# A three-layer CIN on one core: the fifth tile is gathered from the half tables, and the copies into the big table are issued later

## The chip, the cores and the metric

The kernel runs on one core of one Trainium2 chip. Its time is the device time of one execution in microseconds (us). Three executions took 733.25, 734.23 and 734.82 us, so the median before the change is 734.23 us. One further execution was profiled: it took 733.14 us, of which its instructions span 731.4 us; the other 1.74 us lie around the span.

Engines are named as the profile names them: PE is TensorE's matmul, PEld its weight load, DVE is VectorE, ACT ScalarE, POOL GpSimd and SP SyncE. SP computes nothing here; it only issues transfers.

## What is computed

The input x has 1024 samples, 39 fields and 64 embedding columns, in float32. The reference is

```python
def _cin_layer(Xk, X0, W, b):
    O = W.shape[0]
    Hk, Fdim = (Xk.shape[1], X0.shape[1])
    Wr = W.reshape(O, Hk, Fdim)
    return jnp.einsum('bhe,bfe,ohf->boe', Xk, X0, Wr) + b[None, :, None]
X0 = sparse_embedding
Xk = X0
outs = []
for W, b in ((W0, b0), (W1, b1), (W2, b2)):
    Xk = _cin_layer(Xk, X0, W, b)
    outs.append(Xk.sum(axis=-1))
cin_output = jnp.concatenate(outs, axis=-1)
return cin_output @ fc_w.T + fc_b
```

All three layers have 64 outputs. The last layer is only summed and multiplied by a vector, so the kernel folds its weights into a smaller form before the main loop. What is left for the main loop is a matrix product whose rows are the products x_a * x_b of pairs of fields (and x_a alone, which is a pair with a row of ones).

## The kernel before

**Blocks, steps and tiles.** The samples are worked off in 32 blocks of 32 samples. A block has 2048 columns (32 samples by 64 embedding columns). The 39 fields and a row of ones make a table of 40 rows. A pair product needs its two factors in the same partition, so for each block five tiles r of 128 by 2048 are gathered, each an arrangement of table rows on 128 partitions chosen by a list of indices (`lists`). `PAIRS` then names six pairs of tiles, (0,1), (0,2), (3,1), (3,2), (0,4), (3,4): DVE multiplies the two tiles of a pair into a product tile p, and PE multiplies p by the weights. Tile 4, the fifth, is the only one whose list holds row 39, the ones. A seventh, smaller chunk per two blocks takes two small tiles u and v of 128 by 1024.

A step is one such chunk, written (n, c): block n, chunk c. The list `steps` has (0,0) to (0,6), then (1,0) to (1,5), then (2,0) and so on, 13 for every two blocks. Counting from zero, (0,6) is step 6, (1,0) step 7, (1,4) step 11. Chunk 6 is the small one (line 221 on DVE, lines 579 and 590 on PE); all others are line 219 on DVE (128 by 2048 in one instruction, except for the first four steps, which are made by halves or quarters) and line 559 on PE.

**Order of work.** The order of each engine is written out by hand. DVE makes the product of step k+4 after PE has been given step k (`AHEAD = 4`); there are four p buffers, so DVE is at most four steps ahead. When a block is complete, `finish` puts two ACT and four DVE operations and two reductions (lines 607, 609, 620) between the products.

**Tables.** The gathers read tables in device memory. `xd[0]`, `xd[1]`, `xd[2]` hold two blocks each (2 times 40 rows of 2048 columns), in rotation; rows 39 and 79 hold ones. A table is filled from x by `load` (312 KB, pieces of 256 bytes) for each of its blocks, and by `fill_ones`. For the very first block there are two half tables, `xh[0]` and `xh[1]`, of 39 rows by 1024 columns, loaded on ACT's queue by `load_half`; tiles 0 to 3 of block 0 are gathered from these by halves. Tile 4 of block 0, the u and v tiles, and all of block 1 come from `xd[0]`. Its rows for block 0 are copied from the half tables by two transfers on SP's queue (line 396), its rows for block 1 are loaded from x by `load(1, nc.gpsimd)`.

**Queues.** POOL issues all gathers in program order (line 174): eight from the half tables with `load(1)` between the sixth and the seventh, then tile 4 of block 0, then `roll_small(0)` (u and v), then `roll(1)` (five tiles of block 1), then five small transfers of biases and a fill of ones for `xd[2]`, later the gathers of block 2 and so on. The gathers of u, v and block 1 read rows of `xd[0]`, so they wait until the copies, `load(1)` and the ones have landed. SP issues, in this order: the row of fc weights, the two copies (line 396), a fill of ones into `xd[1]`, `load(2)`, `load(3)`, and later the loads of the other blocks. The weights of chunk c are made by `weight_rows(c)` on DVE and ACT and transposed by `weight_turn(c)` on PE, with a copy by ACT (lines 543 to 545).

Of the kernel before, what the change touches and what calls it, by code (L numbers as in the profile page):

```python
# [54 lines left out]
F32 = mybir.dt.float32  # L55
# [5 lines left out]
B, F, E, H = 1024, 39, 64, 64  # L61
FH = F * H
FT = F + 1
# [3 lines left out]
NT = 5  # L67
# [9 lines left out]
SUB = 1024  # L77
# [6 lines left out]
SB = SUB // E  # L84
NBLK = B // BB
NTAB = 3
NY = 3
# [60 lines left out]
def cin_kernel(ctx: ExitStack, tc: tile.TileContext, x, w0t, b0, w1, b1, w2, b2, fc_w, fc_b, out):  # L148
    nc = tc.nc
# [3 lines left out]
    const = ctx.enter_context(tc.tile_pool(name="const", bufs=1))  # L153
    dram = ctx.enter_context(tc.tile_pool(name="dram", bufs=1, space=DRAM))
# [3 lines left out]

    xv = x.rearrange("b f e -> f b e")
    xd = [dram.tile([2 * FT, BLK], F32, name=f"xd{k}") for k in range(NTAB)]  # L160
    xh = [dram.tile([F, SUB], F32, name=f"xh{k}") for k in range(2)]

    def bank(name):
        return psum.tile([128, MM], F32, name=name, tag="po")

    def load(n, engine=nc.sync):
        first = n % 2 * FT
        engine.dma_start(  # L168
            xd[n // 2 % NTAB][first : first + F].rearrange("f (b e) -> f b e", e=E),
            xv[:, n * BB : (n + 1) * BB, :],  # L170
        )

    def gather_rows(dst, table, k):
        nc.gpsimd.indirect_dma_start(  # L174
            dst, None, table, bass.IndirectOffsetOnAxis(ap=lists[:, k : k + 1], axis=0)
        )

    def roll(n, tiles=range(NT)):
        for i in tiles:
            k = n % 2 * NT + i  # L180
            gather_rows(rt[n % 2][:, i], xd[n // 2 % NTAB][: FT if k < NT else 2 * FT], k)

    def roll_small(n):
        table = xd[n // 2 % NTAB].rearrange("f (t c) -> (f t) c", c=SUB)
        for k, dst in enumerate((ut, vt)):
            gather_rows(dst[n // 2 % 2], table, 2 * NT + k)
# [6 lines left out]
    b2s = const.tile([H, 1], F32, name="b2s")  # L193
    b1s = const.tile([128, 1], F32, name="b1s")
    b0s = const.tile([128, 1], F32, name="b0s")
    fc0s = columns[:, 1:2]
    fcb = const.tile([NY * 32, 1], F32, name="fcb")
# [4 lines left out]
    rt = [const.tile([128, NT, BLK], F32, name=f"r{k}") for k in range(2)]  # L202
# [2 lines left out]

    ones = const.tile([16, 2, 128], F32, name="ones")
    ones1 = const.tile([16, 2, 128], F32, name="ones1")

    both = const.tile([128, F * FT], F32, name="both")
    pairs = const.tile([128, NCHUNK, 128], F32, name="pairs")  # L210
# [2 lines left out]
    def product(n, c, cols=slice(0, BLK), p=None):  # L213
        if p is None:
            p = prods.tile([128, BLK], F32, name="p", tag="p")
        if c < NPAIR:
            i, k = PAIRS[c]
            r = rt[n % 2]
            nc.vector.tensor_tensor(p[:, cols], r[:, i, cols], r[:, k, cols], ALU.mult)  # L219
        else:  # L220
            nc.vector.tensor_tensor(p[:, 0:SUB], ut[n // 2 % 2], vt[n // 2 % 2], ALU.mult)  # L221
        return p

    prep = tc.tile_pool(name="prep", bufs=1)
    with prep as prep:
# [24 lines left out]
        nc.sync.dma_start(fcrow, fc_w)  # L250
        def load_half(k):
            nc.scalar.dma_start(
                xh[k].rearrange("f (b e) -> b f e", e=E), x[k * SB : (k + 1) * SB]
            )

        nc.scalar.dma_start(w2s, w2.rearrange("o (s n) -> (o s) n", s=2))
        load_half(0)
        nc.scalar.dma_start(w0s, w0t.rearrange("b (s a) h -> (b s) (a h)", s=NW))
        nc.scalar.dma_start(w1s, w1.rearrange("o (s n) -> (o s) n", s=2))
# [35 lines left out]
        def new():  # L295
            used[0] += 1
            return tmp[:, used[0] - 1 : used[0]]
# [14 lines left out]
        for i in range(NT):  # L312
            at = OFFSET[i] - 3 * K + (0 if i < NT - 1 else -F)
# [54 lines left out]
        def fill_ones(k, engine, src):  # L368
            engine.dma_start(xd[k][F::FT].rearrange("r (p c) -> p r c", c=128), src)

        fill_ones(0, nc.gpsimd, ones)


        nc.vector.tensor_scalar(unit, apart, 0, None, ALU.is_equal)
        for h in (0, H):
            rows = slice(h, h + H)
# [3 lines left out]
        r, most, seat, far = (new() for _ in range(4))  # L380
# [8 lines left out]
        halves = [slice(0, SUB), slice(SUB, BLK)]  # L389
        for k, cols in enumerate(halves):  # L390
            for i in range(4):
                gather_rows(rt[0][:, i, cols], xh[k], i)
                if k and i == 1:
                    load(1, nc.gpsimd)
        for k in (1, 0):
            nc.sync.dma_start(xd[0][0:F, halves[k]], xh[k])
        roll(0, (4,))

# [70 lines left out]
        nc.vector.tensor_tensor(both_of[:, 0:1], most, jumps[:, 0:1], ALU.add)  # L471
        nc.vector.tensor_tensor(both_of[:, 1:2], both_of[:, 0:1], jumps[:, 1:2], ALU.add)
        nc.vector.tensor_scalar(lists[:, 2 * NT :], both_of, 2.0, seat, ALU.mult, ALU.add)
        roll_small(0)
        roll(1)
        for h in (0, H):
            nc.gpsimd.dma_start(b0s[h : h + H], b0.rearrange("(h o) -> h o", o=1))
        nc.gpsimd.dma_start(b1s, b1.rearrange("(h o) -> h o", o=1).to_broadcast([H, 2]))
        nc.gpsimd.dma_start(b2s, b2.rearrange("(h o) -> h o", o=1))
        nc.gpsimd.dma_start(  # L480
            fcb, fc_b.rearrange("(p o) -> p o", o=1).to_broadcast([NY * 32, 1])
        )
        fill_ones(2, nc.gpsimd, ones)
        w1v = w1s.rearrange("o (h f) -> o h f", f=F)
        groups = [(k, min(NA * k, F - NA)) for k in range(4)]
        for k, a in groups:
# [43 lines left out]
    def spread(c):  # L530
        for n in (SQUARE, 2 * SQUARE):
            nc.scalar.copy(pairs[:, c, n : 2 * n], pairs[:, c, 0:n])
# [3 lines left out]
    def weight_turn(c):  # L536
        place = len(turned) % 4 * 128
        if not place:
            tr = bank("tr")
        else:  # L540
            tr = turned[-1]
        turned.append(tr)
        nc.tensor.transpose(tr[:, place : place + 128], pairs[:, c], unit)  # L543
        nc.scalar.copy(wa[:, c, 0 : 2 * H], tr[:, place : place + 2 * H])  # L544
        nc.scalar.copy(wa[:, c, 2 * H :], tr[:, place : place + H])
# [5 lines left out]
    def open_block(n):  # L551
        if n not in po:
            po[n] = [bank("po") for _ in range(BLK // MM)]

    def multiply(n, c, p, quarters=range(BLK // MM)):
        open_block(n)
        for m in quarters:
            side = m % 2 * H
            nc.tensor.matmul(  # L559
                po[n][m],  # L560
                wa[:, c, side : side + 2 * H],
                p[:, bass.ts(m, MM)],
                start=n % 2 == 0 and c == 0,
                stop=n % 2 == 1 and c == NPAIR - 1,
            )
# [32 lines left out]
    def fields(n):  # L598
        g[n] = []
        for m in range(BLK // SUB):  # L600
            gt = work.tile([H + F, SUB], F32, name="g", tag="g")
            nc.scalar.copy(gt[H : H + F], rt[n % 2][0:F, 0, bass.ts(m, SUB)])  # L602
            g[n].append(gt)
# [56 lines left out]
    p = {}  # L660
# [18 lines left out]
    n, c = steps[3]  # L679
    weight_rows(c)  # L680
    p[n, c] = product(n, c, halves[0])
    product(n, c, halves[1], p[n, c])
    for k, (n, c) in enumerate(steps[:3]):
        multiply(n, c, p[n, c], (0,))
        if k < 2:
            weight_turn(steps[k + 1][1])
        multiply(n, c, p[n, c], (1,))

    for at, (n, c) in enumerate(steps[:-TAIL]):
        if c == 0 and 2 <= n and n + 4 < NBLK:  # L690
            load(n + 4)
        quarters = range(BLK // MM)
        if at < 3:
            quarters = quarters[2:]
        if at < NPAIR and at > 1:
            multiply(n, c, p[n, c], quarters[:1])
            weight_turn(steps[at + 1][1])
            quarters = quarters[1:]
            if at == NPAIR - 1:
                multiply(n, c, p[n, c], quarters[:2])  # L700
                weight_turn(NPAIR + 1)
                quarters = quarters[2:]
        if c == NPAIR:
            join(n, p.pop((n, c)))
        else:
            multiply(n, c, p.pop((n, c)), quarters)
        if not at:
            fields(0)
            nc.scalar.copy(ones1, ones)
            fill_ones(1, nc.sync, ones1)  # L710
            for k in (2, 3):
                load(k)
        if at == NPAIR - 2:
            weight_rows(NPAIR + 1)
            for k in (NPAIR, NPAIR + 1):
                spread(k)
        if at - 1 in over:
            finish(over[at - 1])
            fields(over[at - 1] + 1)
        if at + AHEAD < len(steps):  # L720
            n, c = steps[at + AHEAD]
            if at + AHEAD <= NPAIR:
                weight_rows(c)
            p[n, c] = product(n, c)
            if c == NPAIR - 1 and n + 2 < NBLK:
                roll(n + 2)
                if n % 2 == 0:
                    roll_small(n + 2)
                if n < 2:
                    load(n + 4, nc.gpsimd)  # L730
# [75 lines left out]
```

## Time and profile before

| what | value |
|---|---|
| profiled execution: its time / its span | 733.14 us / 731.4 us |
| median of three executions (lowest, highest) | 734.23 us (733.25, 734.82) |
| PE busy | 724.7 us, 99% of the span |
| DVE busy | 638.3 us, 87% |
| POOL busy | 397.6 us, 54% |
| ACT busy | 166.9 us, 23% |
| line 559: instructions, mean of one | 1536, 594 ns |
| line 219: instructions, mean of one | 198, 2224 ns |
| gathers of r from the big tables: count, mean on POOL | 156, 1938 ns |
| gathers of r from the half tables: count, mean on POOL | 8, 996 ns |

Busy times are unions over one engine. Matmuls are pipelined, so the mean of one instruction is longer than the distance from one to the next: in the main loop an instruction of line 559 follows another after 0.431 us (96 in 41.40 us), and a step of line 559 is 8 instructions, 3.45 us. In a line of a timeline stand the start, the time taken, the engine, the line, the operation, what is written from what, a count, and in brackets the time for which the engine stood idle before it and what ended that. POOL's time for a gather is the time in which it writes the transfer's descriptors; the data land later.

### The profile page before, as it was taken

The numbers are of one execution on the slowest core, as the hardware profiler recorded it, in microseconds if no ns is written. First come the engines' busy times: TensorE is split into PE (matmuls) and PEld (weight loads), VectorE is DVE, ScalarE is ACT, GpSimd is POOL, SyncE is SP. The second block draws the span as 40 slices with busy tenths as digits, with TensorE's granted clock in tenths as the row PEclk, the third lists the DMA queues.
The fourth block names the chain that finished last, engine by engine and source line by source line (L and its number), as shares of the span: only waits on it lengthen the run. The fifth ranks groups of instructions, "written<-read, shape, count | busy, mean of one in ns | idle before, by whom it ended". The sixth has DMA issues, their size and how long they took to land.

```text
span 731.4 us, 6351 instructions
## 1 busy us (share of the span) xinstructions
PE 724.7 (99%) x2375; PEld 316.1 (43%) x2375; DVE 638.3 (87%) x521; ACT 166.9 (23%) x240; POOL 397.6 (54%) x254
## 2 busy tenths in 40 slices
PE   8999999999999999999999999999999999999998
PEld 4444444444444444444444444444444444444443
DVE  6999798988889988889988889888898988889885
ACT  3332121222212222221222212222121221212222
POOL 6789886536555445754537555455654547545300
PEclk9999999999999999999999999999999999999999
DMA  8997899789575887757679675896767777565700
GB/s 268 376 337 280 315 342 356 290 307 338 232 273 231 281 336 286 270 225 285 269 288 330 223 289 219 304 348 236 268 256 274 301 287 266 224 252 236 288 0 0
DMA packets 65983, 197.24 MB, mean 270 GB/s; under 512 B 40110, under 2 KB 40179, under 8 KB 45984
## 3 DMA queue, kind: packets, MB, share of 16 engines
q0 software_dynamic: 28784, 185.56, 65.5%
q1 hardware_dynamic: 35468, 9.29, 5.5%
q10 hardware_dynamic: 1700, 1.99, 1.0%
q8 instruction: 18, 0.29, 0.1%
q14 instruction: 13, 0.11, 0.0%
HBM read 196.76 MB, written 10.60 MB: 284 GB/s over the span
## 4 chain that ended last, share of the span: by engine, by line
PE 99%; DVE 0%; DMA 0%; issue 0%; ACT 0%; DVEq 0%
PE po L559 91%; PE po L579 4%; PE po L590 2%; PE idle L279 0%; PE pv L406 0%; PE pt L487 0%; PE small L323 0%; PE pv L487 0%; PE pw L418 0%; DMA fcrow<-in_fc_w 0%; PE tr L543 0%; DVE g L609 0%; DVE pairs L526 0%; DVE sums L631 0%; ACT z L607 0%
## 5 line engine op out<-in xcount | busy, mean ns | idle before, releaser
L559 PE MATMUL po<-p,wa 128*128 128x512 f32 x1536 | 666.0, 594 | 0.0
L219 DVE TENSOR_TENSOR p<-r 128x2048 f32<-128x2048 f32 (+2 forms) x198 | 434.1, 2224 | 72.4 <-PE po L559 67.1
L559 PEld LDWEIGHTS po<-p,wa 128*128 128x128 f32 x1536 | 290.5, 190 | 371.7 <-issue 354.6
L174 POOL DMA_INDIRECT r<-xd,lists x156 | 302.3, 1938 | 267.1 <-issue 266.2
L607 ACT ACTIVATE z<-po,columns 64x512 f32<-64x512 f32 x128 | 87.3, 682 | 380.1 <-PE po L590 217.9
L609 DVE SCALAR_TENSOR_TENSOR g<-po,b0s,z 64x512 f32<-64x512 f32 x128 | 95.9, 749 | 9.3 <-ACT z L607 5.3
L602 ACT COPY g<-r 39x1024 f32<-39x1024 f32 x64 | 66.7, 1043 | 155.0 <-DVE sums L620 126.8
L620 DVE TENSOR_REDUCE sums<-g 103x16 f32<-103x1024 f32 x62 | 75.6, 1220 | 2.1
L174 POOL DMA_INDIRECT u<-xd,lists x16 | 38.9, 2432 | 7.5 <-issue 4.6
L174 POOL DMA_INDIRECT v<-xd,lists x16 | 38.5, 2403 | 4.9 <-issue 4.9
L579 PE MATMUL po<-p,wa 32*64 32x512 f32 x512 | 31.6, 600 | 0.0
L221 DVE TENSOR_TENSOR p<-u,v 128x1024 f32<-128x1024 f32 x16 | 19.5, 1218 | 0.0
L579 PEld LDWEIGHTS po<-p,wa 32*64 32x64 f32 x512 | 9.4, 131 | 20.2 <-issue 19.4
L590 PE MATMUL po<-u,wa 32*64 32x512 f32 x256 | 17.0, 587 | 0.0
L174 POOL DMA_INDIRECT r<-xh,lists x8 | 8.0, 996 | 4.8 <-DVE tmp L387 2.7
L590 PEld LDWEIGHTS po<-u,wa 32*64 32x64 f32 x256 | 5.7, 132 | 8.0 <-issue 8.0
L526 DVE TENSOR_TENSOR pairs<-both 128x2 f32<-128x2 f32 (+27 forms) x59 | 6.1, 171 | 0.2
L544 ACT COPY wa<-tr 128x128 f32<-128x128 f32 x8 | 2.1, 266 | 16.2 <-PE tr L543 16.2
L279 PE MATMUL idle<-const-float32-1.0 128*128 128x256 f32 (+1 forms) x8 | 4.0, 596 | 0.8 <-PEq L793 0.8
L543 PE MATMUL tr<-unit,pairs 128*128 128x128 f32 x8 | 2.4, 294 | 2.2 <-DVE pairs L526 2.2
L543 PEld LDWEIGHTS tr<-unit,pairs 128*128 128x128 f32 x8 | 1.2, 151 | 4.7 <-ACT pairs L524 2.7
L168 POOL DMA_DIRECT2D xd<-in_x x3 | 3.2, 1055 | 0.0
(97 smaller groups left out, 56.7 us busy)
## 6 DMA issues: line engine op xcount, KB each, us to landing
xd<-in_x SPq DMA_DIRECT2D x28, 312.0 KB
r<-xd,lists POOLq DMA_INDIRECT x156, 8.9
xd<-in_x POOLq DMA_DIRECT2D x3, 312.0 KB, 7.6
w2s<-in_w ACTq DMA_DIRECT2D x1, 624.0 KB
w1s<-in_w ACTq DMA_DIRECT2D x1, 624.0 KB
w0s<-in_w0t ACTq DMA_DIRECT2D x1, 380.2 KB
xh<-in_x ACTq DMA_DIRECT2D x2, 156.0 KB
xd<-xh SPq DMA_DIRECT2D x2, 156.0 KB
```

Source lines behind the costliest of these rows:

```text
L174: nc.gpsimd.indirect_dma_start(dst, None, table, bass.IndirectOffsetOnAxis(ap=lists[:, k : k + 1], axis=0))
L219: nc.vector.tensor_tensor(p[:, cols], r[:, i, cols], r[:, k, cols], ALU.mult)
L221: nc.vector.tensor_tensor(p[:, 0:SUB], ut[n // 2 % 2], vt[n // 2 % 2], ALU.mult)
L279: nc.tensor.matmul(idle[:, 0:cols], nc.const_aps.tensor(1.0, (128, 128), F32), nc.const_aps.tensor(1.0, (128, cols), F32), start=True, sto ...
L526: nc.vector.tensor_tensor(out, diagonal(a, b, sa, sb), diagonal(b, a, sb, sa), ALU.add)
L559: nc.tensor.matmul(po[n][m], wa[:, c, side : side + 2 * H], p[:, bass.ts(m, MM)], start=n % 2 == 0 and c == 0, stop=n % 2 == 1 and c == NP ...
L579: nc.tensor.matmul(dst[half * H : half * H + H], wa[rows, NPAIR, at : at + H], p[rows, bass.ts(side, MM)], start=t >= 2, stop=t < 2 and ha ...
L590: nc.tensor.matmul(dst[half : half + H], wa[rows, NPAIR + 1, H : 2 * H], ut[n // 2 % 2][rows, bass.ts(side, MM)], start=False, stop=t < 2,)
L602: nc.scalar.copy(gt[H : H + F], rt[n % 2][0:F, 0, bass.ts(m, SUB)])
L607: nc.scalar.activation(z[one], po[n][m][other], AF.Identity, bias=fc0s[other])
L609: return lambda: nc.vector.scalar_tensor_tensor(g[n][m // 2][0:H, at], po[n][m][one], b0s[one], z[one], ALU.add, ALU.mult)
L620: nc.vector.tensor_reduce(sums[:, b_at : b_at + SB], g[n][m // 2].rearrange("p (b e) -> p b e", e=E), AX.X, ALU.add,)
```

## The change

The half tables get a fortieth row. POOL fills it with ones in two small transfers, where it had filled the ones of `xd[0]`. Tile 4 of block 0 is then gathered from the half tables, in two halves, and no longer from `xd[0]`. `load(1)` moves behind the eighth gather. The two copies into `xd[0]`, now behind a fill of its ones, move on SP's queue behind a wait: the fill reads `ones0`, a tile that ACT writes after the weights of the second chunk have been turned. What reads `xd[0]`, and what stands behind it on POOL's queue, moves to the same place in the program (`fill_table`). The fill of `xd[1]` and the loads of blocks 2 and 3 are put one step later.

```diff
-    xh = [dram.tile([F, SUB], F32, name=f"xh{k}") for k in range(2)]
+    xh = [dram.tile([FT, SUB], F32, name=f"xh{k}") for k in range(2)]
...
+    ones0 = const.tile([16, 2, 128], F32, name="ones0")
...
-                xh[k].rearrange("f (b e) -> b f e", e=E), x[k * SB : (k + 1) * SB]
+                xh[k][0:F].rearrange("f (b e) -> b f e", e=E), x[k * SB : (k + 1) * SB]
...
-        fill_ones(0, nc.gpsimd, ones)
+        for k in range(2):
+            nc.gpsimd.dma_start(
+                xh[k][F:FT].rearrange("r (p c) -> p r c", c=128), ones[0:8, 0:1]
+            )
...
-                gather_rows(rt[0][:, i, cols], xh[k], i)
-                if k and i == 1:
-                    load(1, nc.gpsimd)
-        for k in (1, 0):
-            nc.sync.dma_start(xd[0][0:F, halves[k]], xh[k])
-        roll(0, (4,))
+                gather_rows(rt[0][:, i, cols], xh[k][0:F], i)
+        load(1, nc.gpsimd)
+        for k, cols in enumerate(halves):
+            gather_rows(rt[0][:, NT - 1, cols], xh[k], NT - 1)
...
-        roll_small(0)
-        roll(1)
-        for h in (0, H):
-            nc.gpsimd.dma_start(b0s[h : h + H], b0.rearrange("(h o) -> h o", o=1))
-        nc.gpsimd.dma_start(b1s, b1.rearrange("(h o) -> h o", o=1).to_broadcast([H, 2]))
-        nc.gpsimd.dma_start(b2s, b2.rearrange("(h o) -> h o", o=1))
-        nc.gpsimd.dma_start(
-            fcb, fc_b.rearrange("(p o) -> p o", o=1).to_broadcast([NY * 32, 1])
-        )
-        fill_ones(2, nc.gpsimd, ones)
...
+    def fill_table():
+        nc.scalar.copy(ones0, ones)
+        fill_ones(0, nc.sync, ones0)
+        for k in (1, 0):
+            nc.sync.dma_start(xd[0][0:F, halves[k]], xh[k][0:F])
+        roll_small(0)
+        roll(1)
+        for h in (0, H):
+            nc.gpsimd.dma_start(b0s[h : h + H], b0.rearrange("(h o) -> h o", o=1))
+        nc.gpsimd.dma_start(b1s, b1.rearrange("(h o) -> h o", o=1).to_broadcast([H, 2]))
+        nc.gpsimd.dma_start(b2s, b2.rearrange("(h o) -> h o", o=1))
+        nc.gpsimd.dma_start(
+            fcb, fc_b.rearrange("(p o) -> p o", o=1).to_broadcast([NY * 32, 1])
+        )
+        fill_ones(2, nc.gpsimd, ones)
+
     for k, (n, c) in enumerate(steps[:3]):
         multiply(n, c, p[n, c], (0,))
         if k < 2:
             weight_turn(steps[k + 1][1])
+        if k == 0:
+            fill_table()
         multiply(n, c, p[n, c], (1,))
...
         if not at:
             fields(0)
+        if at == 1:
             nc.scalar.copy(ones1, ones)
             fill_ones(1, nc.sync, ones1)
             for k in (2, 3):
```

## The prediction

> **What bounds the kernel now.** I read the busy times first, then the chain that ended last, then the timelines of DVE, POOL and SP over the first 64 us, the only stretch that the change touches. Page and chain (start, length, what):
>
> ```profile
> PE 724.7 (99%) x2375; PEld 316.1 (43%) x2375; DVE 638.3 (87%) x521; ACT 166.9 (23%) x240; POOL 397.6 (54%) x254
> ...
> 16.43 0.30 PE tr L543
> 16.73 0.61 PE idle L279 x2
> 17.34 1.82 PE po L559 x2
> ...
> 40.30 1.90 PE po L579 x32
> 42.20 0.86 PE po L590 x16
> 43.06 17.36 PE po L559 x40
> ```
>
> PE sets the time: from 17.34 us it multiplies without a hole. Later work can only cost time, and only if a product comes after PE wants it. PE wants step 6 at 40.3, step 7 at 43.06, and then one step every 8 x 0.431 = 3.45 us, so step 11 at 43.06 + 4 x 3.45 = 56.86.
>
> DVE (start, time, in brackets the idle time before and its cause):
>
> ```profile
> 26.78 2.35 DVE L219 TENSOR_TENSOR p<-r 128x1024 f32<-128x1024 f32 x2
> 29.77 2.28 DVE L219 TENSOR_TENSOR p<-r 128x2048 f32<-128x2048 f32 x1
> 32.88 2.28 DVE L219 TENSOR_TENSOR p<-r 128x2048 f32<-128x2048 f32 x1
> 37.22 2.29 DVE L219 TENSOR_TENSOR p<-r 128x2048 f32<-128x2048 f32 x1 [0.39 <-DMA r<-xd,lists]
> 39.80 2.29 DVE L219 TENSOR_TENSOR p<-r 128x2048 f32<-128x2048 f32 x1 [0.29 <-DMA r<-xd,lists]
> 42.42 4.50 DVE L219 TENSOR_TENSOR p<-r 128x2048 f32<-128x2048 f32 x2 [0.33 <-DMA r<-xd,lists]
> ...
> 52.35 11.09 DVE L219 TENSOR_TENSOR p<-r 128x2048 f32<-128x2048 f32 x5
> ```
>
> Steps 7, 8 and 9 (37.22, 39.80, 42.42) each begin when a gather of block 1 lands. Between 46.84 and 52.35 stands `finish` of block 0, 5.51 us. Step 11 opens the row of 52.35 and is ready at 52.35 + 2.28 = 54.63. So PE's cover is 43.06 - 39.51 = 3.55 us at step 7, but only 56.86 - 54.63 = 2.2 us at step 11: gathers of block 1 may come 2.2 us later for nothing, and not more.
>
> POOL:
>
> ```profile
> 18.65 1.66 POOL L174 DMA_INDIRECT r<-xd,lists  x1 [0.30 <-issue]
> 23.23 0.94 POOL L174 DMA_INDIRECT u<-xd,lists  x1 [2.92 <-DVE p L219]
> 24.47 0.95 POOL L174 DMA_INDIRECT v<-xd,lists  x1 [0.30 <-issue]
> 25.73 0.96 POOL L174 DMA_INDIRECT r<-xd,lists  x1 [0.30 <-issue]
> 27.00 3.09 POOL L174 DMA_INDIRECT r<-xd,lists  x1 [0.30 <-issue]
> 30.39 2.61 POOL L174 DMA_INDIRECT r<-xd,lists  x1 [0.31 <-issue]
> 33.30 2.70 POOL L174 DMA_INDIRECT r<-xd,lists  x1 [0.30 <-issue]
> ```
>
> A gather costs POOL 0.94 us, but three cost about 3. Put beside DVE: they end at 30.09, 33.00 and 36.00, and the DVE products that they fell into end at 29.13, 32.05 and 35.16, each 0.84 to 0.96 earlier. A gather that is issued into a product waits for its end and takes 0.8 to 0.95 us more; between products it takes 0.94. So every gather moved into the stretch of full products (from 29 us on) proceeds at the pace of one per product. The page "SBUF — State Buffer" of the Trainium skill (section "Who interferes with whom") explains why: a DVE instruction with two SBUF inputs holds a read interface that GpSimd needs. The same section infers that such a product does not stall descriptor writing, by which every gather would cost 0.94 us and the shift below would be some 2 us smaller; the three rows say otherwise, and I go by them.
>
> **The change part by part.** The sum is made against the profiled execution, 733.14 us.
>
> *The weights, the first multiplications.* Nothing of PE's, DVE's or ACT's work before 19.8 us changes. The gap before the first multiplication (PE stops at 14.26, starts again at 16.43) is filled by DVE's transposes and weight rows, not by a transfer. Price 0. The cover: first-half gathers land by 18.29, about 2 us before their products; later load(1) and absent copies only make this safer.
>
> *Tile 4 by halves.* One gather becomes two, +0.94 us of POOL, and load(1) (1.06 us) goes behind the eighth. The gathers of tiles 2 and 3 come about 1.1 us earlier, which removes DVE's 0.72 us wait at 23.38. Nobody on PE waited for that, as the chain has no hole: gain 0. Tile 4 is issued by 21.5 to 23.5 and lands 3.6 to 6 us later, before (0,4) at about 29.1. Price 0; bounds 0 to 0.4. The extra fill of ones falls into POOL's idle time before 7.17. Price 0.
>
> *ACT's copy of the ones* is the row of 24.17 moved and doubled, 0.40 us at 19.8; ACT's next work is at 21.75. Price 0.
>
> *The copies.* SP:
>
> ```profile
> 10.13 1.70 SPq L396 DMA_DIRECT2D xd<-xh  x2
> 24.60 0.35 SPq L369 DMA_DIRECT2D xd<-ones  x1
> ```
>
> ACT ends the second chunk's weights at 19.79, `ones0` at 20.2. SP then issues the fill (0.35) and the copies (0.92, 0.73): 20.65 and 21.6. How long they take to land now is not in the trace; before, by the semaphore updates, they landed 5.77 and 6.56 us after their issue, at 15.90 and 17.66, beside full gather traffic. Lower bound: the small fill at 24.60 landed in 4.0 us. So the second copy lands between 25.6 and 28.2. Traffic is again heavy then (tile 4), so I take 28.2. The page "DMA: Bandwidth & Descriptors" of the skill (section "Anatomy of one DMA", a fit for GpSimd's transfers) would give an estimate of 2.0 + 160 KB / 436 KB per us = 2.4 us, the copies at 24, and then no shift worth naming. The row is more than twice that, with the same sizes on the same queue.
>
> *What waits for them.* Behind the u gather on POOL stand v, the five gathers of block 1, the biases and the gathers of block 2. POOL restarts 0.7 to 1.1 us after a landing (42.30 to 43.13, 22.09 to 23.23). So u is issued at about 29 instead of 23.23. There it meets DVE, which without its 0.72 us wait runs (0,3) from 26.1 to 28.4, (0,4) from 29.1 to 31.3, (0,5) from 32.2 to 34.5. Two courses:
>
> (a) u slips past (0,3) and ends at 29.2. v falls into (0,4) and ends at 32.15, the first tile of block 1 into (0,5), 35.3. Alone on the queue a full tile lands 4.1 us after its issue (45.60 to 49.72), and each next one 2.5 us later (55.12, 57.60, 60.07): 39.4, 41.9, 44.4, 47.0. Before, the second landed at 37.10 and the fourth at 42.30. Step 7 is made from 42.0 to 44.3: PE waits 1.25 us. Steps 9 and 10 run from 47.1 to 51.6, `finish` to 57.1, step 11 to 59.4, against 56.86: in all 2.5 us.
>
> (b) u falls into (0,4), ends at 32.15; v at 35.26; then DVE stands idle, waiting for v, and the others go at 1.25 us each. Tiles land at 40.6, 43.1, 45.7, 48.2. Step 6 just holds. Step 7 is ready at 45.5 (2.4 us late), step 11 at 60.6: in all 3.7 us.
>
> I take the middle, 3.1 us. Later steps win this back for DVE (a product takes 2.28 us, PE a step 3.45), not for PE.
>
> *The clock.* In the stretches 13.45 to 16.86 and 16.86 to 20.28:
>
> ```profile
> 13.45:16.86 3.41, 1.23 (x6) 0.55 (x4) 2.81 (x11) 1.63 (x6) 2.98 (x3) 1.00 0.99 330
> 16.86:20.28 3.42, 3.42 (x7) 1.54 (x6) 3.42 (x22) 0.87 (x6) 2.88 (x2) 0.50 1.02 386
> ```
>
> PE (first number after the length) was busy for 1.23 of 3.41 us, and the granted clock (third from the end) was 0.50 in the next 3.42, which costs up to 1.7 us. A wait of 1.25 or 2.4 us at step 7 may do the same. But the second wait then shrinks by as much: (a) 1.25 + 1.7 = 2.95 instead of 2.5, (b) 4.1 instead of 3.7. Half of that 0.4: +0.2. A wait at step 11 that halves the clock is not absorbed: +1.7 at most.
>
> *Loads of blocks 2 and 3* are issued 0.4 us later and run while POOL's queue is starved: 0. The biases follow block 1 and land before `finish` reads them: 0.
>
> Sum: 733.14 + 3.1 + 0.2 = 736.4 us. The median before is 1.09 above the profiled execution; I don't add that, since I put it down to the clock in the first 23 us, and a PE that is late there only uses up part of the wait. The end is set by gathers and DVE.
>
> **Rivals.**
>
> *Not slower: the copies land early.* With the 4.0 us of the fill the second lands at 25.6, u goes at 26.5, through (0,3)'s boundary at 27.2, and the tiles shift by less than about 2.5 us. It decides at u issued before roughly 27.5. Then at most 0.3 us of wait is left, inside the usual spread: 734.3 us. For it: load(1) and the gathers are done earlier. Against it: 5.77 and 6.56 us.
>
> *Faster: the start.* Freed of copies between 14 and 17.7, the first products would have to come early enough to spare the halved stretch, 1.7 us: 734.23 - 1.7 = 732.5. Against it: nothing on the chain there waits for a transfer.
>
> *Slower still: POOL is starved.* At 51.80 a gather took 12.45 us under five products in a row. With DVE's lead gone, products follow without gaps for longer, and a gather of block 2 or 3 held like this costs a further 3 to 4 us: 740. Against it: the DVE stall itself lets POOL in.
>
> **How the numbers follow.** Forecast 736.4, its own range 735.6 (a, no clock loss) to 738.6 (b with 1.7): chance 0.58. Early copies 0.24, starved POOL 0.08, faster start 0.10. Within 0.2% of 734.23, some 1.5 us, a measurement of this kernel can't tell from no change. Slower 0.58 + 0.08 = 0.66, same 0.24, faster 0.10. The range from 733.6 to 738.6 takes in the early copies and leaves out the last two.
>
> **What would show it.** Right: the u gather issued at 28 to 29.5 us on POOL; v and the first tile of block 1 taking over 2 us each; DVE waiting at step 7 for a gather until after 41; PE idle before step 7 and step 11, some 3 us together. Wrong: u issued before 27, or PE without a hole between 40 and 60 us; then the copies' landing was mis-sized. Holes after 64 us would be the starved POOL.

## The result and the profile after

| | before | after |
|---|---|---|
| median of 7 executions (lowest, highest) | 733.27 us (732.62, 734.82) | 737.80 us (736.04, 739.86) |
| ratio of the times, 95% interval | | 1.0058 [1.0041, 1.0074] |
| profiled execution: its time / its span | 733.14 / 731.4 us | 738.95 / 737.1 us |

The changed kernel is slower by 0.41 to 0.74%: more than the 0.2% that can be told from no change. The forecast was 736.4 us, with a range up to 738.6.

The page of the kernel after, the waits of PE (us in total, times, longest), and the timeline of PE:

```profile
PE 726.0 (98%) x2375; PEld 316.6 (43%) x2375; DVE 637.9 (87%) x521; ACT 167.1 (23%) x241; POOL 401.8 (55%) x256
```

```profile
PE po L550 <- DVE p L220: 4.5, 2, 3.7
```

```profile
41.30 1.06 PE L581 MATMUL po<-u,wa 32*64 32x512 f32 x16
46.10 43.16 PE L550 MATMUL po<-p,wa 128*128 128x512 f32 x96 [3.74 <-DVE p L220]
106.74 8.85 PE L550 MATMUL po<-p,wa 128*128 128x512 f32 x20 [0.78 <-DVE p L220]
```

PE, which had no hole in its main loop before, now has two that end with a product: 3.74 us before step 7 (46.10) and 0.78 us at 106.74, before step 24. The granted clock has a second halved stretch just behind the first hole (windows; the length, busy time of PE, PEld, DVE, ACT, POOL, then the clock):

```profile
15.74:19.15 3.41, 3.27 (x7) 1.93 (x8) 3.41 (x16) 0.60 (x5) 2.96 (x3) 0.50 1.00 388
46.46:49.87 3.41, 3.41 (x5) 1.33 (x4) 3.22 (x2) 0.00 (x0) 0.89 (x2) 0.50 0.70 286
```

Half the clock for 3.41 us is 1.71 us of work. PE wanted step 7 at 46.10 - 3.74 = 42.36, where it was 43.06 before: 0.70 gained at the start. So 3.74 + 0.78 + 1.71 - 0.70 = 5.53 of the 5.7 us by which the span grew.

Where the first hole comes from is read from right to left: SP's copies, POOL's gathers, DVE's products of the kernel after.

```profile
20.21 1.77 SPq L679 DMA_DIRECT2D xd<-xh  x2
```

```profile
20.09 3.96 POOL L174 DMA_INDIRECT r<-xh,lists  x1 [0.30 <-issue]
27.38 1.20 POOL L174 DMA_INDIRECT u<-xd,lists  x1 [3.33 <-DVE p L220]
28.88 2.60 POOL L174 DMA_INDIRECT v<-xd,lists  x1 [0.30 <-issue]
31.79 2.70 POOL L174 DMA_INDIRECT r<-xd,lists  x1 [0.30 <-issue]
34.79 0.94 POOL L174 DMA_INDIRECT r<-xd,lists  x1 [0.30 <-issue]
...
58.04 14.63 POOL L174 DMA_INDIRECT u<-xd,lists  x1 [0.31 <-issue]
```

```profile
28.26 2.28 DVE L220 TENSOR_TENSOR p<-r 128x2048 f32<-128x2048 f32 x1
...
31.37 2.28 DVE L220 TENSOR_TENSOR p<-r 128x2048 f32<-128x2048 f32 x1
...
43.75 4.71 DVE L220 TENSOR_TENSOR p<-r 128x2048 f32<-128x2048 f32 x2 [7.70 <-DMA r<-xd,lists]
...
88.53 2.29 DVE L220 TENSOR_TENSOR p<-r 128x2048 f32<-128x2048 f32 x1 [5.49 <-DMA r<-xd,lists]
```

The copies are issued at 20.21 and 21.24 and land, by their semaphore updates, at 26.19 and 26.46. The u gather starts 0.92 us later, 4.15 us after its place before. v ends at 31.48, which is 0.94 after the product of step 4 (30.54); the first tile of block 1 ends at 34.49, 0.84 after the product of step 5 (33.65). That tile and the next land at 41.07 and 43.56, and step 7 is made only then. Further on, the u gather of block 2 stays on POOL for 14.63 us (12.45 before); what stands behind it is late, and DVE waits 5.49 us at 88.53. That is the lead which PE misses at 106.74.

### The profile page after: what moved, and what is told of

It is laid out like the page before. It is cut to its first block, busy times and chain, and to the rows that moved or that the text cites. A ratio compares the mean times of both kernels' runs of the same rounds, so it can differ in the third digit from the quotient of the medians.

```text
span 737.1 us, 6358 instructions
## 1 busy us (share of the span) xinstructions
PE 726.0 (98%) x2375; PEld 316.6 (43%) x2375; DVE 637.9 (87%) x521; ACT 167.1 (23%) x241; POOL 401.8 (55%) x256
## 3 DMA queue, kind: packets, MB, share of 16 engines
q10 hardware_dynamic: 1700, 1.99, 0.9%
## 4 chain that ended last, share of the span: by engine, by line
PE 87%; DMA 5%; POOL 4%; issue 3%; DVE 2%; ACT 0%; SPq 0%; DVEq 0%; POOLq 0%
PE po L550 80%; PE po L570 4%; PE po L581 2%; POOL r L174 2%; DMA b0s<-in_b 2%; DMA r<-xd,lists 2%; POOL u L174 1%; DMA v<-xd,lists 1%; DMA xd<-xh 1%; DVE p L220 1%; DVE g L600 1%; PE idle L280 0%; POOL v L174 0%; PE pv L407 0%; PE pt L478 0%
## 5 line engine op out<-in xcount | busy, mean ns | idle before, releaser
L174 POOL DMA_INDIRECT r<-xd,lists x155 | 309.4, 1996 | 264.6 <-issue 257.1
L174 POOL DMA_INDIRECT u<-xd,lists x16 | 40.4, 2525 | 7.9 <-issue 4.6
L174 POOL DMA_INDIRECT v<-xd,lists x16 | 28.2, 1760 | 4.9 <-issue 4.9
L174 POOL DMA_INDIRECT r<-xh,lists x10 | 13.2, 1319 | 4.7 <-issue 2.8
```

The source lines that it names most:

```text
L174: nc.gpsimd.indirect_dma_start(dst, None, table, bass.IndirectOffsetOnAxis(ap=lists[:, k : k + 1], axis=0))
```

## The experiments

Each was run beside the kernel before on the same chip; the ratios are against that. "u" is the start of the first u gather, "held" the time of block 2's u gather on POOL, "step 7" the start of its product on DVE; holes are PE's waits for DVE after 40 us. "PE" is the start of PE's first transposition of weights for the multiplications, the row that ends the first hole. These five columns are from the one profiled execution of each kernel, the ratio is from all of them.

| kernel | ratio, 95% interval | PE | u | step 7 | holes of PE | held |
|---|---|---|---|---|---|---|
| before | 1 | 16.43 | 23.23 | 37.22 | none | 12.45 |
| after | 1.0058 [1.0041, 1.0074] | 15.88 | 27.38 | 43.75 | 3.74, 0.78 | 14.63 |
| 1 copies early | 1.0062 [1.0038, 1.0085] | 16.11 | 25.87 | 41.66 | 1.34, 1.02, 1.47 | 14.65 |
| 2 load(1) early | 1.0078 [1.0061, 1.0094] | 14.44 | 25.45 | 40.42 | 0.59, 0.94, 1.30 | 14.63 |
| 3 copies after first chunk | 1.0077 [1.0060, 1.0095] | 14.54 | 25.56 | 41.46 | 1.91, 0.83, 1.10 | 14.64 |
| 4 products in halves | 1.0073 [1.0056, 1.0090] | 16.42 | 27.05 | 44.30 | 3.63, 1.22 | 14.64 |
| 5 tile 4 by halves only | 1.0015 [1.0001, 1.0030] | 14.24 | 22.83 | 36.76 | none | 12.43 |
| 6 load(1) late only | 1.0075 [1.0060, 1.0091] | 16.53 | 25.38 | 40.71 | 0.73, 1.62 | 14.64 |
| 7 one input | 1.0028 [1.0017, 1.0038] | 16.56 | 27.00 | 41.63 | 0.76, 0.83, 1.55 | 14.64 |
| 8 spin, on before | 0.9998 [0.9989, 1.0007] | 16.03 | 23.30 | 36.82 | none | 12.43 |
| 9 = 2 + 3 | 1.0040 [1.0024, 1.0056] | 16.26 | 25.53 | 42.97 | 2.39, 0.81, 1.47 | 14.64 |
| 10 = 9 + spin | 1.0046 [1.0029, 1.0063] | 14.13 | 23.61 | 39.53 | 1.11 | 14.65 |
| 11 gap | 1.0050 [1.0032, 1.0068] | 14.25 | 26.01 | 39.40 | 0.19, 0.29, 1.88 | 3.65 |
| 12 gap, on before | 0.9993 [0.9982, 1.0003] | 16.68 | 22.13 | 38.20 | none | 3.64 |

The profiles of 2, 3, 5, 10 and 11 start early. The kernel after, then 5:

```profile
15.88 0.45 PE L534 MATMUL tr<-unit,pairs 128*128 128x128 f32 x1 [2.19 <-DVE pairs L517]
14.24 0.30 PE L538 MATMUL tr<-unit,pairs 128*128 128x128 f32 x1 [2.18 <-DVE pairs L521]
```

The hole is the same, but PE comes to it some 2 us sooner. Its four matmuls into `pt` before it took 1.34 to 1.40 us in these five profiles and 2.29 to 2.36 us in the other nine. The edits are not the cause: 9 has those of 2 and 3 and starts at 16.26. Each of the five is also the fastest execution of its kernel. So u and step 7 of these five can't be set beside those of the others as they stand.

**1. Copies early.** The whole change, but the copies are issued where they were, right behind the gathers.

```diff
-        nc.scalar.copy(ones0, ones)
-        fill_ones(0, nc.sync, ones0)
-        for k in (1, 0):
-            nc.sync.dma_start(xd[0][0:F, halves[k]], xh[k][0:F])
...
             gather_rows(rt[0][:, NT - 1, cols], xh[k], NT - 1)
+        fill_ones(0, nc.sync, ones)
+        for k in (1, 0):
+            nc.sync.dma_start(xd[0][0:F, halves[k]], xh[k][0:F])
```

> The changed kernel, but the fill of the ones and the two copies into the big table are issued on SP as early as before, without the wait for the second chunk's weights; tile 4 by halves and the later load(1) stay. Theory (the late copies hold u, v and block 1's gathers on POOL): u is issued when load(1) has landed, about 25 us instead of 27.4, block 1's tiles come at most 2.2 us later than before, no hole in PE: 733.3 to 735 us. Rival (tile 4 by halves with the later load(1) costs the time): it stays at 737 to 738.5.

Missed: the time stayed, though the copies had landed at 16.93 and 17.88. Kernel 1 on POOL:

```profile
20.32 5.25 POOL L174 DMA_INDIRECT r<-xh,lists  x1 [0.30 <-issue]
25.87 2.95 POOL L174 DMA_INDIRECT u<-xd,lists  x1 [0.30 <-DVE pairs L520]
```

The first row is the second half of tile 4, the gather that the change adds. It meets four products in a row (DVE, 19.98 to 24.60) and holds up u; load(1), issued at 16.39, also lands only at 24.39. So the late copies were not the only thing that made u late.

**2. load(1) early**, back between the sixth and the seventh gather; the copies still wait.

```diff
+                if k and i == 1:
+                    load(1, nc.gpsimd)
-        load(1, nc.gpsimd)
```

> The changed kernel, but load(1) goes back between the sixth and the seventh gather of the half tables. Theory (the copies land last): u still waits for the copies and is issued at 27 to 28 us: 737 to 738.5 us. Rival (u waits for load(1), which the change put back): u goes at about 25 us and the time is 733.3 to 735.

As expected: the copies, issued at 17.94 here, land at 23.7 and 24.54 and hold u until 25.45; nothing is won in the median. That u came before the 27 to 28 us named goes with the early start of this profile.

**3. Copies after the first chunk's weights**, the four lines of `fill_table` moved behind the first `weight_turn(c)` and its `spin()`.

```diff
             weight_turn(c)
             spin()
+            nc.scalar.copy(ones0, ones)
+            fill_ones(0, nc.sync, ones0)
+            for h in (1, 0):
+                nc.sync.dma_start(xd[0][0:F, halves[h]], xh[h][0:F])
```

> The changed kernel, but ones0 is written after the first chunk's weights, so that SP's fill and copies start some 2.4 us earlier, at about 17.2 us. Theory: copies land at about 24 us, u goes at about 25, one product earlier than in the changed kernel: 733.5 to 735.5 us, clearly under it. Rival (the issue time of the copies does not matter as long as they come after the half-table gathers): 737 to 738.5.

Missed: the copies go at 15.96, but load(1), issued at 18.40 and landed at 24.83, holds u instead.

**4. Products in halves**: the products of steps 4 and 5 as two instructions each, to give v and the first tile a boundary in the middle.

```diff
-            p[n, c] = product(n, c)
+            if at + AHEAD in (4, 5):
+                p[n, c] = product(n, c, halves[0])
+                product(n, c, halves[1], p[n, c])
+            else:
+                p[n, c] = product(n, c)
```

> The changed kernel, but DVE makes the products of steps 4 and 5 in two halves of 1024 columns instead of one instruction of 2048. Theory (a gather issued into a product waits for that instruction's end): v ends near 30.2 us instead of 31.5, block 1's first tile 1 to 3 us earlier than 34.5, and the time falls by 1 to 2.5 us, to 735.3 to 736.8. Rival (POOL's 2.6 us gathers come from the transfer queue being full or slow, not from DVE): POOL's times stay, 737.5 to 738.2, the 0.1 us that two more DVE instructions cost included.

Missed: v took 2.67 us and ended at 32.09, 0.95 after the second half's end (31.14); the tile ended 0.84 after its second half. A boundary between two instructions that follow each other at once lets no gather in. What counts is a break in the row (11).

**5 and 6** part the change. 5 has the halves of tile 4 alone: kernel 1 with load(1) as in 2. 6 has the late load(1) alone, in the kernel before:

```diff
-                if k and i == 1:
-                    load(1, nc.gpsimd)
+        load(1, nc.gpsimd)
         for k in (1, 0):
```

> The changed kernel with both moves taken back: copies and ones early on SP as before, load(1) between the sixth and the seventh gather. What is left of the change is tile 4 gathered by halves from the half tables. Theory A (what counts is when u is issued: anything that puts it behind the products of 24 us costs the same 4 to 5 us, whether copies, load(1) or one more gather): u at about 22.5 to 24, step 7 at 37 to 38.5, 733 to 735 us. Theory B (one more gather on POOL is enough by itself, since early copies alone left the time at 737.7): 736.5 to 738.5.

> The kernel before with one part of the change alone: load(1) behind the eighth gather; copies early, tile 4 in one gather from the big table. Theory A: u waits for load(1), which lands 2 to 3 us later, is issued at 25 to 26 us, and its followers meet the products: step 7 at 40 to 42, 736 to 738.5 us. Theory B (late load(1) alone is harmless): 733 to 734.5.

5 came out between its two theories. In the median it is nearly the kernel before, but its ten executions fall into four at 732.8 to 733.3 and six at 735.1 to 737.1 us. The profile is of the first four, and of those that start early: PE was 2.19 us ahead of the kernel before at its first transposition and 0.4 us ahead at the end (span 731.0 against 731.4). What the six lose is not seen. 6 starts like the kernel before and costs as much as the whole change, more than either theory had. Kernel 6 on POOL:

```profile
25.38 0.94 POOL L174 DMA_INDIRECT u<-xd,lists  x1 [4.95 <-DVE p L219]
26.62 2.60 POOL L174 DMA_INDIRECT v<-xd,lists  x1 [0.30 <-issue]
29.53 2.62 POOL L174 DMA_INDIRECT r<-xd,lists  x1 [0.30 <-issue]
32.45 2.70 POOL L174 DMA_INDIRECT r<-xd,lists  x1 [0.30 <-issue]
```

u is only 2.15 us later than before, but it misses the time in which v and the first tile went at 0.95 and 0.96 us. They now take 2.6 each, and the second tile ends at 35.15 instead of 30.09. Step 7 comes 3.49 us later, just inside its cover of 3.55, and PE waits for nothing there. Step 11's product starts at 55.55, 3.2 later against a cover of 2.2, and PE waits 0.73 at 57.89.

**7. One input**: the products of steps 4 and 5 are replaced by a reduction over an axis of one element, of the same size, which reads one tile. Those two products are left out of the computation.

```diff
+            if at + AHEAD in (4, 5):
+                p[n, c] = prods.tile([128, BLK], F32, name="p", tag="p")
+                nc.vector.tensor_reduce(
+                    p[n, c], rt[0][:, PAIRS[c][1]].unsqueeze(2), AX.X, ALU.add
+                )
```

> The changed kernel, but DVE's products of steps 4 and 5 are replaced by a reduction over an axis of one element, which reads one tile instead of two and writes as many columns (the two products are left out of what is computed). DVE is as long busy. Theory (a running product holds back the gathers): v and block 1's first tiles take 0.94 us each on POOL instead of 2.6 and 2.7, step 7 starts at 38 to 41 us instead of 43.75, the time falls to 733.3 to 736. Rival (late copies or a slow queue hold the gathers): POOL's 2.6 us stay, 737 to 738.5.

Kernel 7, POOL, and DVE beside it:

```profile
27.00 2.27 POOL L174 DMA_INDIRECT u<-xd,lists  x1 [0.98 <-DMA xd<-xh]
29.57 0.94 POOL L174 DMA_INDIRECT v<-xd,lists  x1 [0.30 <-issue]
30.82 0.94 POOL L174 DMA_INDIRECT r<-xd,lists  x1 [0.30 <-issue]
```

```profile
29.14 2.29 DVE L737 TENSOR_REDUCE p<-r 128x2048 f32<-128x2048 f32 x1
```

v is issued in the middle of a DVE instruction as long as the product, and takes 0.94 us. So it is the two-input product that holds a gather. About half of the loss is gone, as expected, though step 7 came after the 38 to 41 us named; the interval lies just clear of the changed kernel's.

**8 and 10. Spin**: three more multiplications that nobody reads (`spin(3)`), put before DVE's transposes, to keep PE busy and so spare the halved clock at 16 us; in 8 on the kernel before, in 10 on kernel 9, which joins 2 and 3.

```diff
+        spin(3)
         for k, a in groups:
             nc.vector.transpose(
```

> The kernel before with three more idle matmuls of 256 columns on PE behind the last matmuls of the weights, in the hole from 14.3 to 16.4 us. Theory (the clock is halved after 16.9 us because PE was idle in the stretch before): the stretch after it is granted at 1.0 and the time falls by up to 1.7 us, to 731.6 to 733. Rival (the clock does not follow that hole, or PE is back too late): 733 to 734.

> The changed kernel with both softened: ones0 is written after the first chunk's weights (copies issued near 16 us) and load(1) is back between the sixth and the seventh gather; tile 4 by halves stays. Theory (u's issue decides, and the products that catch u or v make the jump): u at about 23.5 us, near the edge, step 7 at 37 to 40: 733 to 736 us, better than either softening alone (738.5 and 738.6). Rival (any form of the change costs 4 us): 737 to 738.5.

> The same with three more idle matmuls on PE in the hole before the first multiplication, as in the run with the idle matmuls alone. Theory (there PE's gain was lost because DVE waited 1.06 us for a half-table gather, and here that wait is shorter): 0.5 to 1.5 us under the kernel without them, and at best 732 to 733, under the kernel before. Rival: no difference, or slower, because a PE that is early meets the same gathers of block 1.

The clock did as asked. Two windows of kernel 8, columns as above:

```profile
12.68:16.09 3.41, 2.54 (x11) 1.66 (x11) 2.92 (x11) 1.71 (x5) 2.79 (x4) 1.00 0.96 321
16.09:19.50 3.41, 3.29 (x10) 1.38 (x10) 3.41 (x18) 0.96 (x6) 2.80 (x3) 1.00 1.02 405
```

But the time stayed (0.9998): PE, early by 1.0 us at 27.41, then waits for DVE, 0.56 us at 29.96, and DVE had waited 1.06 for a gather at 23.45. In 9 the copies, issued at 17.67, still held u until 25.53. In 10, which starts early, they are issued at 15.55, land in time, and u starts at 23.61, but the gathers from the half tables meet DVE's earlier products: DVE waits 1.99 us for one at 23.24, and PE 1.17 us at 24.5. Both came out as their rivals said: neither gets back to the kernel before.

**11 and 12. Gap**: a memset of one element (0.06 us) behind every product on DVE; in 11 on the changed kernel, in 12 on the kernel before.

```diff
+    gap = const.tile([1, 1], F32, name="gap")
...
+        nc.vector.memset(gap, 0.0)
```

> The changed kernel with a memset of one element on DVE behind every product, so that no two products run without a break. Theory (a gather is let in only where the row of products breaks, and the second wait of PE, near step 24, comes from block 2's u gather being held for 14.6 us by six products in a row): that gather takes 3 to 5 us instead of 14.6, the wait near step 24 is gone, and the time falls by 0.8 to 2.5 us to 735.3 to 737; the wait at step 7 stays, because copies are as late. Rival (the hold does not depend on breaks between products): the 14.6 us stay, 737.5 to 739.

> The kernel before with the same memsets. Theory: the memsets take 0.1 us or less each and lie in DVE's spare time, PE has no hole to lose: within 0.2% of before; block 2's u gather takes 3 to 5 us instead of 12.45. If they cost DVE more than its spare time, it is slower by up to 1%.

Kernel 11 on POOL, the gather that had taken 14.63 us:

```profile
55.30 3.65 POOL L174 DMA_INDIRECT u<-xd,lists  x1 [0.30 <-issue]
```

The hole near step 24 is gone with it, as expected, which shows where that hole came from (2, 3 and 10, which start early too, have it). The wait at step 7, expected to stay, is 0.19 us in this early profile, and a hole of 1.88 us stands at step 11 (58.19). The median is not shown to be better than the changed kernel's (the intervals overlap), and 12, as expected, is not shown to be faster than the kernel before. No version here beats that.

## Why the prediction was right, and where it was not

**Right: the direction and the course.** Slower, by u. The copies took 5.98 and 5.22 us to land, near the rows that were used (5.77, 6.56). They were not near the 2.4 us estimated from the fit for GpSimd's transfers in "DMA: Bandwidth & Descriptors" of the Trainium skill ("Anatomy of one DMA"). u was issued at 27.38, a little before the 28 to 29.5 that was named and after the 27 that would have refuted it. It took course (a): it got in behind step 3, and v and the first tile took 2.60 and 2.70 us. A second stretch of half the clock came, and kernel 7 shows that the two-input products hold the gathers. "SBUF — State Buffer" of the skill ("Who interferes with whom") states this of a GpSimd instruction that reads SBUF; the gathers agree with it, though no run here shows the port itself. Its inference that descriptor writing is not stalled differs from the rows of the gathers. It does not differ from those of plain transfers: in the kernel before, the one at 38.74 took 0.67 us inside the product of 37.22 to 39.51.

**Mis-sized: the wait at step 7.** It was put at 1.25 us (a) to 2.4 (b) and was 3.74. The failed term is the landing. From the end of the first tile's issue to the start of step 7 it took 35.3 to 42.0, 6.7 us, in the prediction, by a tile alone on its queue and the next 2.5 us behind it. It measured 34.49 to 43.75, 9.26 us. By the semaphore updates the first tile landed 6.6 us after the end of its issue, instead of 4.1, and the second 2.5 us behind it, as assumed. In kernel 6 the first took 4.0 us and the second 4.4 more. The row to use stood in the trace of before: there the two took 10.4 us (26.69 to 37.10), though the second's gather was itself held for 3.09 us. What makes the pair slow is not shown. With 9.26 in place of 6.7, course (a) would have given 3.8 us.

**Inside the range partly by luck.** The sum was made against the profiled execution, and there the time grew by 5.8 us, to 738.95, beyond the range's end of 738.6; the median of the kernel after is 1.15 us lower. Too little stood for the wait at step 7, for the clock (1.71 us where 0.2 had been added) and for step 24; against them stand the wait at step 11, 1.25 us or so that did not come, and 0.70 us gained at the start.

**The wait at step 11 did not come, as the step on the clock allowed.** With 1.7 us lost to the clock, PE wanted step 11 at about 46.10 + 1.7 + 4 x 3.45 = 61.6, and its product was ready at 58.58 + 2.28 = 60.9.

**The starved POOL came in part**, on top of the forecast and not as its rival: 14.63 us instead of 12.45, and 0.78 us of hole where 3 to 4 had been priced. Kernel 11 shows the mechanism.

**Wrong, without showing in the sum: three zeros.** "load(1) later: 0" is a loss as large as the change's when it stands alone (6). "Tile 4 by halves: 0" is not far off alone (5, slower by 0.01 to 0.30%), but with load(1) late its second half was held for 5.25 us and kept u back until 25.87 (1), where load(1) alone gives 25.38 (6). Neither part had a cover of its own: each delays u, and the delays lie side by side, so that undoing one leaves the next in its place (1, 2, 3). And the rival "copies land early", with 734.3 us for u at up to 27.5, is refuted: kernels 1 and 6, whose profiles do not start early, have u at 25.87 and 25.38 and are slower by 0.38 to 0.91%. It let the tiles shift by less than u itself; in kernel 6 a delay of 2.15 us became 5.06 at the end of the second tile's issue. Last, "nobody on PE waited" for DVE's wait of 0.72 was true only beside a PE held back by the clock (8).

**Open.** In 2, 3, 5, 6, 10 and 11 the profiled execution is 2.3 to 3.3 us faster than the median of the same kernel; in the kernel before, 8 and 12 it is not. So their holes do not add up to the whole loss. Two things on record account for a part. All of them but 6 start early. And the mean granted clock, which stands beside the time of every execution, is 0.997 in the profile of 6 and 0.995 in its three others; in 11 it is 0.997, and 0.995 in five of seven others; in 2 it is 0.997, and 0.993 to 0.995 in three of four others. A halved stretch of 3.41 us takes 0.002 off this mean, so these executions had at least about one more, 1.7 us. Where it lay isn't seen, and 3 (but for one execution), 5 and 10 do not show it. Whether a late u is the whole cause is open too: in kernel 10 it comes only 0.38 us later than before, but 9.48 us behind PE's first transposition, against 6.80. The late copies alone, with tile 4 still gathered whole, were not tried: that gather reads what they write and would wait for them itself.

## What to carry to other kernels

When a gather is moved, price it and everything behind it by what each will meet at its new time, not by the shift: missing the gaps in a row of two-input products turned 2.15 us into 5.06. Where several things guard one start, ask for each when it lands; undoing the one that comes last only uncovers the next. And take the landing time of a group of transfers from the same group, not from one alone on its queue. Before two profiles are compared, look whether they start alike.

## What was not expected of the hardware

- A gather issued into a row of products was held for up to 14.6 us, as long as the row lasted; a DVE memset of 0.06 us between products cut this to 3.65. A boundary between two halves of a product did not let it in (4).
- The granted clock was halved behind a stretch with PE busy for 1.23 of 3.41 us (before) and kept at 1.00 behind one with 2.54 of 3.41 (kernel 8).
- In five of fourteen profiles the same four matmuls before the main loop took 1.34 to 1.40 us instead of 2.29 to 2.36, and PE's first transposition came some 2 us sooner.
